# Turning four groups of tokens before the first attention step, gate scores from an exponential, and a bias addition tied to its step

## The chip, the core and the metric

The kernel runs on one core of one Trainium2 chip. The core has a matrix engine (TensorE, PE in the profile, with its weight loads as PEld), a vector engine (VectorE, DVE), an engine for activation functions (ScalarE, ACT), a general engine (GpSimd, POOL) and a queue engine that only issues transfers here (SyncE, SP). The metric is the device time of one execution in microseconds, as the median of three runs.

## The reference

The kernel computes one transformer block on a tensor of 4 x 1024 tokens with 256 channels, in float32. Attention and a mixture of experts both read the same normalised input, and both are added to it:

```python
xn = layernorm(x)
x = x + attention(xn) + experts(xn)

def attention(x):                     # 16 heads of 16 channels
    q, k, v = split(x @ W_qkv + b_qkv)
    q, k = rotary(q), rotary(k)
    a = softmax(q @ k.T / sqrt(16))
    return (a @ v) @ W_out + b_out

def experts(x):                       # 16 experts in 4 groups of 4
    scores = sigmoid(x @ w_gate.T)
    # a group's score is the sum of its two best scores; the best 2 groups stay,
    # and of their 8 experts the best 4 (w, idx)
    w = w / (sum(w) + 1e-6)
    routed = sum over the 4: w * (silu(x @ w1_e.T) * (x @ w3_e.T)) @ w2_e.T
    shared = (silu(x @ w1_s.T) * (x @ w3_s.T)) @ w2_s.T
    return routed + shared
```

## The kernel before

**Steps.** The 4096 tokens are 32 tiles of 128, and 8 groups of 4 tiles (`QT = 4`). Attention is the backbone: 256 steps (`STEPS`), 16 for each of 16 pairs of a batch entry and four heads. A step takes four score matmuls `ps` (L1289) through an exponential on ScalarE (`es`, L1298), makes four matmuls `pm` (L1247) whose row maxima (`mx`, L1255, a VectorE reduction) the next pair needs, and multiplies earlier exponentials into the values (`av`, L1314). Four matmuls come in the first half and four in the second; `between()` places all other work of the step, its *units*, in the middle. `max_off` (L1266 to L1275) merges two maxima, transposes them on TensorE (`pmt`) and subtracts them from the queries (`q2`). Until it has run, a pair's exponentials can't begin.

**Before step 0.** Groups 0 and 1 are normalised and transposed (`turn`, L467 to L492: four transposes per half group on TensorE into a PSUM bank `pt`, one copy on ScalarE), the first batch entry's queries, keys and values are made in eight tiles, and the first maxima are taken: `max_round(0, 0, s)` for eight `s`. The even ones run within the tile loop, the odd ones after it. Meanwhile ScalarE and VectorE collect statistics of groups 2 to 7, and POOL turns them into scale and offset (`rstd`, `off`). `scale(q)` (L456) is four ScalarE activations that normalise group `q` in place.

**Groups 2 to 7.** `Norm.moves(step)` runs at the head of a step: it scales group `step + 3`, stores the rows of group `step + 2` to DRAM (`xnd`) and, from group 4, the transposed group to `xnTd`. `Norm.pieces(step)` puts the turns of group `step + 2` among the units, and in steps 3 and 5 the gate's matmuls for groups 2 to 5 and 6 and 7 (`pg`, L502). Their logits come a step later (`plg`, L518). In steps 0 to 6 the own pair's remaining maxima are units too.

**Routing.** `route` is a generator. From step 9 (`ROUTE_FROM`) it is advanced three times in a step, twice while the experts are ranked, and each advance runs to the next `yield`. It begins with the sigmoid of all logits (L608, 128x512) and the best two of each group (`hi`, `lo`, L616 and L618). `rank` (L630 to L637) compares with VectorE (`ge`, two buffers) and adds and subtracts on POOL (`rk`, L635 and L636) for 15 distances.

**Shared experts.** `shared_block` makes units for 16 blocks of 256 tokens. `gate(1)` holds a POOL addition of the output bias to the block's input rows `xb` (L875), which `last` uses two units later (L905). The rows are loaded by SP well ahead (`early_x`).

**Who sets the order.** A planner orders each engine's instructions by simulated readiness, unless they are tied. `keep_in_program_order` ties one behind everything traced so far on its engine, and all TensorE work and all SP transfers of `k.sp` are tied in this way. `issue_after(ins)` queues behind `ins` on its engine. `paced` adds a true wait on `k.pace`, the latest reduction or exponential that a step's hooks have passed. PSUM has eight banks from one pool (`k.bank`), and SBUF buffers are reused by tag.

Of the kernel before, what the change touches and what calls it, by code (L numbers as in the profile page):

```python
# [10 lines left out]
AF = mybir.ActivationFunctionType  # L11
# [9 lines left out]
NT = B * TT  # L21
# [7 lines left out]
HALF = 512  # L29
QT = 4  # L30
# [22 lines left out]
def kernel(  # L53
# [23 lines left out]
    nc = tc.nc  # L77
# [6 lines left out]
    k = Kit(tc, banks)  # L84
# [35 lines left out]
    logits = rt_pool.tile([P, NT, E], F32, name="logits", tag="logits")  # L120

    ff = ctx.enter_context(tc.tile_pool(name="ff", bufs=2))
    norm = Norm(k, att, ff, keep, logits, power)
# [44 lines left out]
    with tc.issue_after(k.rotary):  # L168
        for power_of in powers:
            power_of()  # L170
    norm.scale(2)
    for qt in range(4):
        att.max_round(0, 0, 2 * qt + 1)
    att.max_off(0, 0, 0)

    def weights():
        nc.scalar.dma_start(out=k.w1s_sb, in_=w1s.rearrange("(c p) f -> p c f", p=P))
        nc.scalar.dma_start(out=k.w3s_sb, in_=w3s.rearrange("(c p) f -> p c f", p=P))
        nc.scalar.dma_start(out=k.w2s_sb, in_=w2s.rearrange("(c p) h -> p c h", p=P))
        k.sp(wout_sb, w_out.rearrange("(c p) f -> p c f", p=P))  # L180
# [115 lines left out]
class Kit:  # L296


    def __init__(self, tc, banks):
        self.tc, self.nc, self.banks = tc, tc.nc, banks  # L300
        self.last_sp = self.last_exp = None
        self.ranking = self.slots_known = False
        self.summed = self.shared_rows = 0
# [26 lines left out]
class Norm:  # L330
# [3 lines left out]
    def __init__(self, k, att, ff, keep, logits, power):  # L334
        self.k, self.nc, self.att, self.ff = k, k.nc, att, ff
        self.logits, self.power = logits, power
        self.gates = {3: (2, 3, 4, 5), 5: (6, 7)}
        self.less = keep.tile([P, NT], F32, name="less")
        self.sq = keep.tile([P, NT], F32, name="sq")
        self.x4, self.xnT, self.part, self.lg = {}, {}, {}, {}  # L340
        self.mv, self.rstd, self.off, self.scaled = {}, {}, {}, None
# [28 lines left out]
    def power_of(self, q):  # L370
        nc, ff, mv = self.nc, self.ff, self.mv[q]
        rstd = self.rstd[q] = ff.tile([P, QT], F32, name=f"rstd_{q}", tag="rstd", bufs=8)
        keep = self.k.tc.keep_in_program_order
        keep(nc.gpsimd.tensor_scalar_add(mv[:, :, 1], mv[:, :, 1], 1e-5))
        keep(nc.gpsimd.tensor_tensor(rstd, mv[:, :, 1], self.power, ALU.pow))
# [76 lines left out]
    def scale(self, q):  # L452
        nc = self.nc
        for i in range(QT):
            x = self.x4[q][:, i, :]
            scale = nc.scalar.activation(  # L456
                x, x, AF.Identity,
                bias=self.off[q][:, i : i + 1], scale=self.rstd[q][:, i : i + 1],
            )
            if q < 4:  # L460
                self.k.tc.keep_in_program_order(scale)

    def store(self, q):
# [3 lines left out]
    def turn(self, q, pair):  # L467

        nc, k = self.nc, self.k
        b, hf = divmod(q, 2)  # L470
        if hf == 0 and pair == 0 and b < 2:
            self.xnT[b] = k.xnTp.tile([P, NC_, T], F32, name=f"xnT_{b}", tag="xnT")
        if pair == 0:
            if b < 2:
                self.part[q] = self.xnT[b][:, :, hf * HALF : (hf + 1) * HALF]
            else:

                self.part[q] = self.att.one.tile(
                    [P, NC_, HALF], F32, name=f"xnTq_{q}", tag=("oc", "acc")[hf]
                )  # L480
        pt = k.bank([P, NC_, 2, P], f"pt_{q}_{pair}")
        for i in range(2):
            for c in range(NC_):
                k.pe(
                    nc.tensor.transpose(  # L485
                        pt[:, c, i, :], self.x4[q][:, 2 * pair + i, c * P : (c + 1) * P], k.ident
                    )
                )
        nc.scalar.copy(
            self.part[q][:, :, pair * 2 * P : (pair + 1) * 2 * P],  # L490
            pt.rearrange("p c i n -> p c (i n)"),
        )  # L492

    def gate(self, qs):

# [35 lines left out]
    def moves(self, step):  # L531

        k = self.k
        q = step + 3
        if q < NT // QT:
            with k.tc.issue_after(k.last_exp or k.pace):
                self.scale(q)
        if step + 2 < NT // QT:
            self.store(step + 2)
        if 4 <= step + 1 < NT // QT:  # L540
            b, hf = divmod(step + 1, 2)
            k.sp(k.xnTd[b][:, :, hf * HALF : (hf + 1) * HALF], self.part[step + 1])

    def pieces(self, step, own):
        out = []
        if step + 2 < NT // QT:
            out += [lambda: self.turn(step + 2, 0), lambda: self.turn(step + 2, 1)]
        if own:
            out.append(own.pop(0))
        if step in self.gates:  # L550
            out.append(lambda: self.gate(self.gates[step]))
        if step - 1 in self.gates:
            out.append(lambda: self.logits_of(self.gates[step - 1]))
        return out + own


def route(k, one, logits, tensor):
# [5 lines left out]
    nc = k.nc  # L563
# [7 lines left out]
    with k.tc.issue_after(k.rotary):  # L571
# [3 lines left out]
            out=before, in_=before, compare_op=ALU.is_gt, fill=0.0, base=0,  # L575
# [20 lines left out]
        out=same, in_=k.ident.rearrange("p (t e) -> p e t", e=E), axis=AX.X, op=ALU.add  # L596
# [6 lines left out]
        out=late, in_=late, compare_op=ALU.is_gt, fill=0.0, base=-E * shift,  # L603
# [1 line left out]
    )  # L605

    sc = tile_([P, NT, E], "sc")
    k.tc.keep_in_program_order(nc.scalar.activation(sc, logits, AF.Sigmoid))  # L608
    yield


# [104 lines left out]
    while not ahead:  # L716
# [23 lines left out]
        out=lower, in_=lower, compare_op=ALU.is_gt, fill=0.0, base=0,  # L740
# [53 lines left out]
class Beside:  # L794
# [52 lines left out]
    def shared_block(self, blk):  # L847


        k, nc = self.k, self.nc  # L850
        b, at = divmod(blk * SL, T)
        st = {"gu": []}

        def half(c, n):
            ph = k.bank([P, SL], f"ph_s{blk}_{c}_{n}")
            w = (k.w1s_sb, k.w3s_sb)[n]
            for i in range(NC_):
                k.pe(
                    nc.tensor.matmul(  # L859
                        ph, lhsT=w[:, i, c * P : (c + 1) * P],  # L860
                        rhs=self.xnT[b][:, i, at : at + SL],
                        start=(i == 0), stop=(i == NC_ - 1),
                    )
                )
            return ph

        def gate(c):
            def run():
                if c == 0:
                    self.early_x(blk)  # L870
                    if blk + 1 not in (SHARED_FIRST, NT // R):
                        self.early_x(blk + 1)
                    st["x"] = self.xb[blk]
                else:
                    nc.gpsimd.tensor_tensor(  # L875
                        st["x"], st["x"], k.bo_sb.unsqueeze(1).to_broadcast([P, R, C]), ALU.add
                    )
                if at == 0 and c == 0:
                    self.want(b)
                ph = half(c, 0)  # L880
                th = st["th"] = self.ff.tile([P, SL], F32, name=f"th_s{blk}_{c}", tag="th")
                nc.scalar.activation(th, ph, AF.Tanh, scale=0.5)
                nc.vector.scalar_tensor_tensor(th, th, 1.0, ph, ALU.add, ALU.mult)
            return run

        def up(c):
            def run():
                ph = half(c, 1)
                gu = self.ff.tile([P, SL], F32, name=f"gu_s{blk}_{c}", tag="gu", bufs=3)
                nc.vector.tensor_tensor(gu, st["th"], ph, ALU.mult)  # L890
                st["gu"].append(gu)
            return run

        def last(r):
            def run():
                po = k.bank([P, C], f"pso_{blk}_{r}")
                for c in range(FS // P):
                    k.pe(
                        nc.tensor.matmul(  # L899
                            po, lhsT=st["gu"][c][:, r * P : (r + 1) * P], rhs=k.w2s_sb[:, c, :],  # L900
                            start=(c == 0), stop=(c == FS // P - 1),
                        )
                    )
                x = st["x"][:, r, :]
                nc.vector.scalar_tensor_tensor(x, po, 0.5, x, ALU.mult, ALU.add)  # L905
                if r == R - 1:
                    self.later.append(store)
            return run

        def store():  # L910
            k.sp(k.rows(k.acc, blk * R, R), st["x"])
            k.shared_rows = (blk + 1) * R

        return [gate(0), up(0), gate(1), up(1)] + [last(r) for r in range(R)]
# [655 lines left out]
```

## Time and profile before

| | us |
|---|---|
| median of three runs | 1413.76 |
| lowest and highest run | 1411.64, 1413.96 |
| the profiled execution | 1414.77 |
| its span, first to last instruction | 1413.1 |

The profiled execution's span leaves out 1.7 us of its time that lie around the instructions. Rows of the timeline begin with the start and the duration in us, then the engine, the line in the kernel, the operation, what it writes and reads with shapes, and how many instructions were merged; in brackets stands how long the engine was idle before, and what released it. Rows of the windows table begin with the stretch of time. A kind like `qkT` is a buffer that several tensors share: groups 2 to 5 lie in buffers of the queries and keys that are needed only later. `granted clock` is the share of full speed that TensorE was allowed.

### The profile page before, as it was taken

The numbers are of one execution on the slowest core, as the hardware profiler recorded it, in microseconds if no ns is written. First come the engines' busy times: TensorE is split into PE (matmuls) and PEld (weight loads), VectorE is DVE, ScalarE is ACT, GpSimd is POOL, SyncE is SP. The second block draws the span as 40 slices with busy tenths as digits, with TensorE's granted clock in tenths as the row PEclk, the third lists the DMA queues.
The fourth block names the chain that finished last, engine by engine and source line by source line (L and its number), as shares of the span: only waits on it lengthen the run. The fifth ranks groups of instructions, "written<-read, shape, count | busy, mean of one in ns | idle before, by whom it ended". The sixth has DMA issues, their size and how long they took to land.

```text
span 1413.1 us, 25832 instructions
## 1 busy us (share of the span) xinstructions
PE 1389.0 (98%) x9446; PEld 653.6 (46%) x9446; DVE 931.0 (66%) x1734; ACT 783.6 (55%) x1586; POOL 424.7 (30%) x498
## 2 busy tenths in 40 slices
PE   7899999999999999999999999999999999999998
PEld 4443333343343335566566665665664333333333
DVE  6778758778777765444555555555447988998941
ACT  4564445565555555555555555555555555555575
POOL 5401603764444454220000000002225444444400
PEclk9899999999999999999999999999999999999999
DMA  5143743413332333547666666665432434433310
GB/s 187 45 150 134 283 165 104 142 68 105 120 120 104 99 135 95 172 153 230 210 203 201 202 202 213 197 200 174 150 120 75 125 107 128 127 108 105 109 38 31
DMA packets 136670, 199.10 MB, mean 141 GB/s; under 512 B 13920, under 2 KB 99040, under 8 KB 136288
## 3 DMA queue, kind: packets, MB, share of 16 engines
q1 hardware_dynamic: 103088, 137.78, 30.7%
q0 software_dynamic: 12288, 33.57, 7.7%
q10 hardware_dynamic: 21168, 26.10, 5.3%
q8 instruction: 75, 1.23, 0.4%
q14 instruction: 51, 0.42, 0.1%
HBM read 124.01 MB, written 79.69 MB: 144 GB/s over the span
## 4 chain that ended last, share of the span: by engine, by line
PE 97%; DVE 1%; DMA 1%; ACT 1%; issue 0%; POOL 0%; ACTq 0%; POOLq 0%; DVEq 0%
PE ps L1289 20%; PE pm L1247 20%; PE av L1314 18%; PE ph_r L827 9%; PE exy L994 5%; PE ph_s L859 5%; PE pqk L1161 4%; PE py L1383 2%; PE pso L899 2%; PE pv L1161 2%; PE ext L985 2%; PE ptr L1228 2%; PE pmt L1270 1%; PE po L1338 1%; DVE mx L1255 1%; PE pt L485 1%
## 5 line engine op out<-in xcount | busy, mean ns | idle before, releaser
L1298 ACT ACTIVATE es<-ps 128x512 f32<-128x512 f32 x1024 | 554.9, 596 | 460.3 <-PE ps L1289 238.4
L1255 DVE TENSOR_REDUCE mx<-pm 128x1 f32<-128x512 f32 x1024 | 661.3, 685 | 193.9 <-PE pm L1247 139.0
L1247 PE MATMUL pm<-kT,qT 32*128 32x512 f32 x1792 | 513.1, 646 | 1.4 <-ACT kT L1233 1.4
L1289 PE MATMUL ps<-q,kT 32*128 32x512 f32 x1792 | 509.3, 643 | 3.1 <-DVE mx L1255 2.2
L1314 PE MATMUL av<-es,vv 128*32 128x512 f32 (+1 forms) x2144 | 277.3, 588 | 0.0
L1289 PEld LDWEIGHTS ps<-q,kT 32*128 32x128 f32 x1792 | 142.5, 184 | 192.5 <-ACT es L1298 135.0
L1247 PEld LDWEIGHTS pm<-kT,qT 32*128 32x128 f32 x1792 | 147.5, 185 | 67.6 <-DVE mx L1255 30.0
L835 DVE SCALAR_TENSOR_TENSOR th_r<-th_r,ph_r 128x256 f32<-128x256 f32 x72 | 30.3, 421 | 199.6 <-ACT th_r L834 199.6
L950 POOL DMA_INDIRECT xs<-rows,slot_i x128 | 124.0, 969 | 114.7 <-DVE mx L1255 101.5
L1042 POOL DMA_INDIRECT yg<-ys,slot_i x128 | 121.5, 949 | 121.8 <-DVE mx L1255 115.8
L1192 POOL TENSOR_TENSOR rot<-qk,sin_sb 128x256 f32<-128x256 f32 x56 | 39.5, 728 | 348.4 <-DVE qk L1149 348.2
L827 PE MATMUL ph_r<-xT,w 128*128 128x128 f32 x1152 | 140.5, 275 | 0.5 <-ACT xT L988 0.5
L1314 PEld LDWEIGHTS av<-es,vv 128*32 128x32 f32 x2144 | 43.1, 108 | 199.9 <-issue 178.1
L827 PEld LDWEIGHTS ph_r<-xT,w 128*128 128x128 f32 x1152 | 134.4, 192 | 0.8 <-ACT xT L988 0.7
L994 PE MATMUL exy<-w,gu_r 128*128 128x256 f32 x288 | 76.6, 388 | 0.0
L834 ACT ACTIVATE th_r<-ph_r 128x256 f32<-128x256 f32 x72 | 27.7, 384 | 82.6 <-PE ph_r L827 82.6
L1289 PE MATMUL ps<-q,qkT 32*128 32x512 f32 x256 | 72.7, 640 | 0.0
L1247 PE MATMUL pm<-qkT,qkT 32*128 32x512 f32 x256 | 72.6, 640 | 0.0
L994 PEld LDWEIGHTS exy<-w,gu_r 128*128 128x128 f32 x288 | 50.6, 190 | 28.9 <-issue 21.7
L1059 DVE SCALAR_TENSOR_TENSOR sum<-yg,wk,sum 128x256 f32<-128x256 f32 x128 | 63.6, 496 | 0.4 <-DMA yg<-ys,slot_i 0.4
L1000 ACT ACTIVATE y<-exy 128x512 f32<-128x512 f32 x72 | 43.2, 600 | 35.0 <-PE exy L994 29.9
L875 POOL TENSOR_TENSOR xb<-xb,bo_sb 128x512 f32<-128x512 f32 x16 | 20.9, 1308 | 90.4 <-DMA xb<-in_x_dram 76.4
(178 smaller groups left out, 1210.3 us busy)
## 6 DMA issues: line engine op xcount, KB each, us to landing
w<-we SPq DMA_DIRECT2D x144, 384.0 KB, 3.8
xs<-zero ACTq DMA_DIRECT2D x8, 2304.0 KB, 7.9
xg<-xs SPq DMA_DIRECT2D x72, 256.0 KB, 4.8
ys<-y SPq DMA_DIRECT2D x72, 256.0 KB, 4.7
acc<-acc SPq DMA_DIRECT2D x14, 512.0 KB, 5.2
xb<-in_x_dram SPq DMA_DIRECT2D x16, 256.0 KB, 4.2
acc<-xb SPq DMA_DIRECT2D x16, 256.0 KB, 3.2
we<-in_w_dram ACTq DMA_DIRECT2D x4, 1024.0 KB, 7.3
```

Of the source, the lines that this page charges most:

```text
L827: nc.tensor.matmul(ph[:, n, at], lhsT=w[n][:, c, :], rhs=xT[:, c, at], start=(c == 0), stop=(c == NC_ - 1),)
L859: nc.tensor.matmul(ph, lhsT=w[:, i, c * P : (c + 1) * P], rhs=self.xnT[b][:, i, at : at + SL], start=(i == 0), stop=(i == NC_ - 1),)
L950: put = nc.gpsimd.indirect_dma_start(out=k.xs, out_offset=bass.IndirectOffsetOnAxis(ap=k.slot_i[:, t, kk : kk + 1], axis=0), in_=self.rows ...
L994: nc.tensor.matmul(py[:, r, :], lhsT=gus[i][:, r * P : (r + 1) * P], rhs=got[i][1][:, r, 2 * NC_ * F :], start=True, stop=True,)
L1042: get = nc.gpsimd.indirect_dma_start(out=self.yg[:, kk, :], out_offset=None, in_=k.ys, in_offset=bass.IndirectOffsetOnAxis(ap=k.slot_i[:, ...
L1059: nc.vector.scalar_tensor_tensor(sm[:, 0, :], yg[:, kk, :], k.wk[:, t, kk : kk + 1], sm[:, 0, :], ALU.mult, ALU.add)
L1161: nc.tensor.matmul(ps, lhsT=self.xnT[b][:, c, t * P : (t + 1) * P], rhs=self.wqkv_sb[:, c, at : at + w], start=(c == 0), stop=(c == NC_ - 1),)
L1247: nc.tensor.matmul(ps, lhsT=self.qT[b, g // 2][rows, g % 2, qt * P : (qt + 1) * P], rhs=self.kT[b, g // 2][rows, g % 2, hf * HALF : (hf + ...
L1255: k.pace = nc.vector.tensor_reduce(out=self.mx_of[b, g, qt // 4][hf][:, qt % 4, j, :], in_=ps, axis=AX.X, op=ALU.max,).ins
L1289: nc.tensor.matmul(ps, lhsT=self.kT[b, g // 2][rows, g % 2, kc * P : (kc + 1) * P], rhs=self.q2[b, g, qh][rows, :], start=True, stop=True,)
L1298: k.last_exp = nc.scalar.activation(e, ps, AF.Exp, scale=DH**-0.5).ins
L1314: nc.tensor.matmul(av[32 * j : 32 * j + 32, cols], lhsT=self.vv[b][:, kc, h * VS : h * VS + 32], rhs=es[j][:, cols], start=(kc == 0), stop ...
```

## The change

The turns of groups 2 to 5, with the scalings of groups 3 to 5, move before step 0, between and behind the odd rounds of the first maxima; their scalings and copies are tied into ScalarE's order. Groups 6 and 7 are scaled at steps 0 and 1 and turned in steps 2 and 3, the gate's matmuls move to steps 1 and 4, and the stores of transposed groups 4 to 7 to steps 0, 1, 3 and 4. The gate's scores are computed as 1 / (1 + exp(-logit)) by an exponential on ScalarE, an addition and a reciprocal on VectorE; four yields are added. The bias's addition waits for the step's pace instruction.

```diff
     norm.scale(2)
+    norm.scale(3)
+
     for qt in range(4):
         att.max_round(0, 0, 2 * qt + 1)
+        if qt == 1:
+            norm.turn(2, 0)
+            norm.scale(4)
+        if qt == 2:
+            norm.turn(2, 1)
+    for q in (3, 4):
+        for pair in range(2):
+            norm.turn(q, pair)
+    norm.scale(5)
     att.max_off(0, 0, 0)
+    for pair in range(2):
+        norm.turn(5, pair)
...
-        self.gates = {3: (2, 3, 4, 5), 5: (6, 7)}
+
+        self.turns, self.gates = {2: 6, 3: 7}, {1: (2, 3, 4, 5), 4: (6, 7)}
...
-            if q < 4:
+            if q < 6:
                 self.k.tc.keep_in_program_order(scale)
...
-        nc.scalar.copy(
+        copy = nc.scalar.copy(
             self.part[q][:, :, pair * 2 * P : (pair + 1) * 2 * P],
             pt.rearrange("p c i n -> p c (i n)"),
         )
+        if 2 <= q < 6:
+            k.tc.keep_in_program_order(copy)
...
-        q = step + 3
+        q = step + 6
         if q < NT // QT:
             with k.tc.issue_after(k.last_exp or k.pace):
                 self.scale(q)
         if step + 2 < NT // QT:
             self.store(step + 2)
-        if 4 <= step + 1 < NT // QT:
-            b, hf = divmod(step + 1, 2)
-            k.sp(k.xnTd[b][:, :, hf * HALF : (hf + 1) * HALF], self.part[step + 1])
+        q = step + 4 if step < 2 else self.turns.get(step - 1)
+        if q:
+            b, hf = divmod(q, 2)
+            k.sp(k.xnTd[b][:, :, hf * HALF : (hf + 1) * HALF], self.part[q])
...
-        if step + 2 < NT // QT:
-            out += [lambda: self.turn(step + 2, 0), lambda: self.turn(step + 2, 1)]
+        if step in self.turns:
+            out += [lambda i=i: self.turn(self.turns[step], i) for i in range(2)]
...
-    k.tc.keep_in_program_order(nc.scalar.activation(sc, logits, AF.Sigmoid))
+    k.tc.keep_in_program_order(nc.scalar.activation(sc, logits, AF.Exp, scale=-1.0))
+    yield
+    yield
+    yield
+    nc.vector.tensor_scalar_add(sc, sc, 1.0)
+    yield
+    nc.vector.reciprocal(sc, sc)
     yield
...
-                    nc.gpsimd.tensor_tensor(
+                    plus = nc.gpsimd.tensor_tensor(
                         st["x"], st["x"], k.bo_sb.unsqueeze(1).to_broadcast([P, R, C]), ALU.add
                     )
+                    k.paced(plus.ins)
```

## The prediction

> **What bounds the kernel now.** I read the page's busy shares first, then TensorE by stage (windows), then its waits, then the timelines around each bad stage.
>
> ```profile
> PE 1389.0 (98%) x9446; PEld 653.6 (46%) x9446; DVE 931.0 (66%) x1734; ACT 783.6 (55%) x1586; POOL 424.7 (30%) x498
> 46.00:61.00 15.00, 9.91 (x42) 4.44 (x40) 12.52 (x22) 6.18 (x17) 10.77 (x46) 0.76 0.28 88
> 120.00:142.00 22.00, 20.79 (x112) 6.98 (x105) 17.64 (x42) 12.42 (x21) 5.13 (x4) 0.84 0.58 214
> 168.00:182.00 14.00, 11.80 (x68) 3.74 (x68) 7.46 (x17) 4.84 (x9) 4.60 (x11) 0.88 0.61 221
> 182.00:300.00 118.00, 118.00 (x730) 45.91 (x734) 87.65 (x149) 63.81 (x131) 50.56 (x51) 1.00 0.41 135
> ```
>
> The columns are the window, its length, busy us of PE, PEld, DVE, ACT and POOL, then the granted clock. From 182 us on TensorE is busy at clock 1.00, and nothing edited there is on its path. The change can pay only in three stages: 46 to 112 us (first maxima and steps 0 to 6), 120 to 142 (gate scores, steps 9 to 12), 168 to 182 (step 19).
>
> ```profile
> 48.06 4.12 ACT L456 ACTIVATE qkT<-qkT,off,rstd 128x256 f32<-128x256 f32 x8
> 49.18 9.66 DVE L1255 TENSOR_REDUCE mx<-pm 128x1 f32<-128x512 f32 x16 [1.16 <-PE pm L1247]
> 59.12 1.12 PE L1270 MATMUL pmt<-ident,mx 128*128 128x128 f32 x4 [2.93 <-DVE mx L1266]
> 61.08 1.22 PE L1289 MATMUL ps<-q,kT 32*128 32x512 f32 x1 [0.85 <-DVE q L1275]
> 54.00:56.00 2.00, 2.00 (x5) 0.50 (x2) 2.00 (x5) 0.00 (x0) 1.75 (x6) 0.50 0.85 244
> 64.00:66.00 2.00, 2.00 (x10) 1.19 (x12) 0.52 (x1) 1.43 (x3) 0.00 (x0) 0.50 0.00 0
> ```
>
> In the first stage the sixteen reductions set the pace (9.66 us, 0.604 each), ScalarE is idle after 52.2, and the clock is halved from about 53.8 to 67.4.
>
> ```profile
> 121.47 1.28 ACT L608 ACT_TABLE_LOAD   x1
> 122.76 0.63 ACT L608 ACTIVATE sc<-logits 128x512 f32<-128x512 f32 x1
> 123.41 1.28 ACT L1298 ACT_TABLE_LOAD   x1
> 124.71 2.56 ACT L1298 ACTIVATE es<-ps 128x512 f32<-128x512 f32 x5
> 124.25 2.88 POOL L875 TENSOR_TENSOR xb<-xb,bo_sb 128x512 f32<-128x512 f32 x2
> 124.52 1.49 DVE L618 TENSOR_TENSOR lo<-sc 128x256 f32<-128x256 f32 x1
> 171.91 1.26 POOL L875 TENSOR_TENSOR xb<-xb,bo_sb 128x512 f32<-128x512 f32 x1 [5.37 <-DMA xb<-in_x_dram]
> 175.06 1.12 PE L1289 MATMUL ps<-q,kT 32*128 32x512 f32 x2 [2.20 <-DVE mx L1255]
> ```
>
> Two table loads surround the sigmoid, and five exponentials pile up behind them. Two early bias additions on POOL stretch `lo` (its twin `hi` took 0.42). At 166.5 POOL stands 5.4 us behind a bias addition whose rows have not landed, with the ranks of L635 queued behind it. VectorE then waits for a rank buffer, and TensorE for VectorE.
>
> **Part one, the turns.** Nothing disappears; work moves. One group costs four scalings (2.06 us on ACT, half of the row of eight), eight transposes (1.09 on TensorE when warm, 1.97 when cold) and two copies (1.07 on ACT). Groups 2 to 5 leave steps 0, 1, 2, 3, and groups 6 and 7 go from steps 4, 5 to 2, 3.
>
> New stretch before step 0, from 48.06: ACT scales groups 2 and 3 to 52.2 as now, copies (52.8), scales group 4 (its offset is ready at 52.6) to 54.9, makes five copies to about 58.3 and scales group 5 to 60.4. TensorE has all matmuls of the maxima out by about 55.5, since 8 PSUM banks hold at most 8 results and ACT frees the turns' banks. The reductions should therefore still end at 58.84. All turns but group 5's hide under them. Group 5's stand between the maxima's transposes and step 0, ending about 61.7: step 0 begins 0.6 late. Without that cover the four groups would cost 4 x 1.97 on TensorE and more on ACT.
>
> Steps 0 to 6 start now at 61.1, 68.1, 75.7, 82.1, 89.3, 97.3 and 104.1, and step 7 at 111.9 (first `ps` of each in the timeline): 50.8 us. I rebuild each from warm pieces: a half step 1.07, full `av` 1.06, own round of maxima 1.15 (VectorE: eight reductions, 4.83), gate 1.92, logits 0.66. Step 0 cold without its turn: 5.9; step 1 with the gate 6.4; step 2 with turn and logits 6.2; step 3 with turn 5.6; step 4 with gate 6.4; step 5 5.4; step 6, twelve reductions, 7.5. Sum 43.4, so 7.4 saved, less the 0.6: **6.8**. Only 4.4 of it is TensorE work; the rest is scalings that now stand between exponentials in steps 1 to 4. Lower end 3.0, if those stalls come back as VectorE backlog. Upper end 8.5.
>
> A rule bears against this. The Trainium skill, "TensorE: Matmul & The Clock Gate", part on PE-mode transpose, says that transposes do not count as PE activity for the clock. Row 54:56 agrees with the general idea (PE 2.00 of 2.00 busy, clock 0.50), but shows thin matmuls and not transposes. If transposes counted, step 0 could start warm and about 2 us more would come. I follow the rule and leave step 0 cold.
>
> DMAs: the stores of groups 4 and 5 to `xnTd` go out at steps 0 and 1, those of 6 and 7 at steps 3 and 4. SP takes them in order, and store(3) and `wout_sb` stand behind them, some 10 us before `fold` needs the latter: nothing. On POOL the powers stay in place.
>
> **Part two, the gate scores.** Two loads of 1.28 leave ACT: 2.6. "ScalarE: Activation LUTs", What ACT_TABLE_LOAD costs, puts a drain of 1.38 beside each load, which would make 5.3 for two switches. The trace has the next ACTIVATE 1.29 and 1.30 after each load, so I take 2.6. VectorE gains an addition (0.42, as the 128x512 TENSOR_SCALAR of L664) and a 128x512 reciprocal that no row shows. RECIPROCAL took 250 ns at 128x16 and 343 at 128x32: 5.8 ns per element, hence 343 + 480 x 5.8 = 3.1. Ends: 0.7 (an ordinary pass of that width) and 5.5 (16 times the row of 32); I take 3.1, the slope. It stands in step 10 between reductions, and the rest of routing slips four yields.
>
> Steps 9 to 12 take 22.4 now (119.7 to 142.1; steps 10 and 11 alone 13.7, mostly cold). After: step 9 4.3. Steps 10 and 11: VectorE has eight reductions 5.2, addition and reciprocal 3.5, nine small passes and `q` 3.6, 12.3 in all; TensorE runs ahead by the free banks, about 2 us: 10.3. Step 12 5.1. One cold window of 3.4 costs 1.2. Sum 20.9, gain 1.5; the long reciprocal would turn it into a loss of 1. I take **1.0**, range -3 to 4.
>
> **Part three, the bias's addition.** The added wait is on the step's pace instruction, a reduction or an exponential that has just been issued; behind it on POOL stand that step's ranks, later the row puts, which TensorE does not wait for. Block 2's addition leaves step 19: the stall of 2.2 goes, and the cold window after it (176.6 to 180.0, half speed: 1.7): **3.6**, leaving 0.3 to what is late next. Block 0's addition comes into step 14, where now three rank rounds fall together (7.6 us of POOL for the first three in the trace, plus 1.3). Ranks have two buffers, so VectorE waits near step 15, some 2.6 less the banks' slack: **loss 1.0**, range 0 to 3. The other additions run beside a VectorE that is 66% busy: nothing.
>
> **Sum.** 6.8 + 1.0 + 3.6 - 1.0 = 10.4. The profiled execution took 1414.8 (span 1413.1), 1.0 above the median of 1413.8: 1404.4 on its scale, **1403.4** on the median's.
>
> **Rivals.** (a) As above, 0.60: 1400 to 1407. (b) The moved work buys only its TensorE time and VectorE becomes the bound, 0.20: 4.4 - 0.6 from turns, -2 for the reciprocal with two cold windows, 3.6 - 1.0: 4.4, so 1409.4. For it: reductions already end the wait of `ps` and `pmt`. Against: VectorE is 66% busy, and ACT has 29.9 us of work in 61 to 112. (c) Slower, 0.12: POOL holds VectorE off at every tied addition. `lo` lost 1.07 beside one, and sixteen now sit within busy steps. All of it on TensorE's path would be 17.1, less 10.4: 1420.5. It cancels the gain from 0.65 each and shows as slower from 0.83. Against: from 182 us on, thirteen additions run today without a TensorE wait. (d) The planner had the order so already, or the added ties bring other waits as large as the ones removed, 0.08: 1413.
>
> About 0.2% (2.8 us) is what a measurement can tell from no change. Faster: all of (a), most of (b): 0.79. Same: the rest of (b), most of (d) and the mild end of (c): 0.11. Slower: 0.10. Leaving out the low end and (c) gives 1399.5 to 1412.
>
> **What would show it.** Right: step 7 starts near 105 on the old scale; four L456 groups before 61; no table load at the gate; one RECIPROCAL of about 3 us; L875 after its step's ranks and no 2.2 us wait at step 19. Wrong: reductions of the first stage with gaps, `ps` of step 0 later than 63, clock 0.5 over more than one window in steps 10 to 12, or POOL's L875 in front of a late reduction in many steps.

## The result and the profile after

| | before | after |
|---|---|---|
| median of the runs of this comparison, us | 1412.70 (4 runs) | 1420.87 (4 runs) |
| lowest and highest run, us | 1411.53, 1413.96 | 1420.32, 1421.18 |
| profiled execution, us | 1414.77 | 1420.75 |
| its span, us | 1413.1 | 1419.0 |

The ratio is 1.0054, with a 95% interval of 1.004 to 1.0067. The changed kernel is slower, by about 8 us; a gain of 10 was forecast.

The page's busy shares hardly move. The windows do (window, length, busy time of PE, PEld, DVE, ACT and POOL, granted clock, DMA share, GB/s):

```profile
PE 1384.9 (98%) x9454; PEld 651.4 (46%) x9454; DVE 933.3 (66%) x1736; ACT 781.8 (55%) x1584; POOL 425.6 (30%) x498
46.00:61.00 15.00, 1.14 (x9) 0.86 (x8) 2.52 (x5) 4.37 (x14) 10.93 (x45) 0.69 0.00 0
179.00:193.00 14.00, 14.00 (x92) 5.06 (x88) 10.47 (x23) 7.00 (x13) 4.05 (x11) 1.00 0.81 290
```

Between 46 and 61 us TensorE now works 1.14 us of 15, where it worked 9.91. The last row is the stage around step 19, which the changed kernel reaches 11 us later (180.9 for 169.8): TensorE is busy throughout, where it worked 11.80 us of 14. TensorE's waits name the cause of the first; the fields are the engine, what it waited to write, whom for, us in total, times and the longest. The first line is of before, the others are of after:

```profile
PE pm L1247 <- ACT kT L1233: 1.4, 1, 1.4
...
PE pm L1271 <- ACT kT L1257: 14.5, 1, 14.5
PE pmt L1294 <- DVE mx L1290: 1.4, 1, 1.4
PE po L1362 <- DVE q L1299: 1.1, 1, 1.1
PE ps L1313 <- DVE mx L1279: 0.9, 1, 0.9
```

The wait for ScalarE's copy `kT` has grown from 1.4 us to 14.5. The timeline of ScalarE, with one row of POOL ahead of it, says what the copy stood behind:

```profile
56.40 0.20 POOL L435 TENSOR_TENSOR off<-less,rstd 128x4 f32<-128x4 f32 x1
...
56.63 1.09 ACT L470 ACTIVATE x<-x,off,rstd 128x256 f32<-128x256 f32 x2 [11.06 <-POOL off L435]
57.63 0.62 ACT L1257 COPY qT<-ptr 128x256 f32<-128x256 f32 x2
58.15 0.65 ACT L1257 COPY kT<-ptr 128x256 f32<-128x256 f32 x2
...
59.67 1.09 ACT L470 ACTIVATE x<-x,off,rstd 128x256 f32<-128x256 f32 x2
60.65 0.64 ACT L1257 COPY qT<-ptr 128x256 f32<-128x256 f32 x2
61.17 0.67 ACT L1257 COPY kT<-ptr 128x256 f32<-128x256 f32 x2
```

L470 is `scale`, and its rows that write `x` and not `qkT` belong here to group 6. Two of its four activations stand ahead of one tile's query and key copies, two ahead of the next tile's. The first pair waits 11.06 us for group 6's offset, which POOL has only at 56.6. The queries and keys of the last two tiles stand behind it, and behind those the whole first stage. On TensorE:

```profile
61.62 3.79 PE L1271 MATMUL pm<-kT,qT 32*128 32x512 f32 x16 [14.48 <-ACT kT L1257]
...
73.66 0.66 PE L1294 MATMUL pmt<-ident,mx 128*128 128x128 f32 x4 [1.39 <-DVE mx L1290]
74.15 1.35 PE L499 MATMUL pt<-ident,qkT 128*128 128x128 f32 x8
75.42 0.69 PE L1313 MATMUL ps<-q,kT 32*128 32x512 f32 x1
```

Step 0 begins at 75.42, not 61.08: **14.3 us late**. That is more than the whole loss.

To follow the rest I use one mark every eight steps, the start of ScalarE's copy `oT`; the first falls in step 9. Relative to the first profile of before, after stands at +6.96 in step 9, +10.61 in step 17, +6.79 in step 25 and +5.98 at the last mark. So steps 0 to 8 won back 7.4 of the 14.3, steps 9 to 17 lost 3.7, steps 18 to 25 won 3.8, and 0.8 more came late. In the gate's stage the new rows on VectorE, TensorE and POOL are these:

```profile
133.59 3.34 DVE L631 RECIPROCAL sc<-sc 128x512 f32<-128x512 f32 x1
...
137.54 0.66 PE L1362 MATMUL po<-ident,oT 128*128 128x128 f32 x4 [1.15 <-DVE q L1299]
...
160.09 1.27 POOL L898 TENSOR_TENSOR xb<-xb,bo_sb 128x512 f32<-128x512 f32 x1
...
163.90 0.56 DVE L657 TENSOR_TENSOR ge_e<-msk 128x384 f32<-128x384 f32 x1 [0.90 <-POOL rk L659]
...
165.12 1.12 PE L1313 MATMUL ps<-q,kT 32*128 32x512 f32 x2 [0.94 <-DVE mx L1279]
```

While the reciprocal runs, `q` waits for VectorE, and TensorE waits for `q`. Later block 0's addition stands between the first two rank rounds, VectorE waits 0.90 for a rank buffer, and TensorE 0.94 for VectorE.

### The profile page after: what moved, and what is told of

Its sections match the earlier page's. It is cut to its first block, busy times and chain, and to the rows that moved or that the text cites. A ratio compares the mean times of both kernels' runs of the same rounds, so it can differ in the third digit from the quotient of the medians.

```text
span 1419.0 us, 25853 instructions
## 1 busy us (share of the span) xinstructions
PE 1384.9 (98%) x9454; PEld 651.4 (46%) x9454; DVE 933.3 (66%) x1736; ACT 781.8 (55%) x1584; POOL 425.6 (30%) x498
## 4 chain that ended last, share of the span: by engine, by line
PE 95%; DVE 2%; POOL 1%; ACT 1%; DMA 0%; issue 0%; ACTq 0%; DVEq 0%; POOLq 0%
PE pm L1271 20%; PE ps L1313 20%; PE av L1338 18%; PE ph_r L850 9%; PE exy L1018 5%; PE ph_s L882 4%; PE pqk L1185 4%; PE pso L923 2%; PE py L1407 2%; PE ext L1009 2%; PE pv L1185 2%; PE ptr L1252 2%; PE po L1362 1%; PE pmt L1294 1%; PE pf L1395 1%; PE pt L499 1%
## 5 line engine op out<-in xcount | busy, mean ns | idle before, releaser
L1271 PE MATMUL pm<-kT,qT 32*128 32x512 f32 x1792 | 510.7, 644 | 14.6 <-ACT kT L1257 14.5
L1083 DVE SCALAR_TENSOR_TENSOR sum<-yg,wk,sum 128x256 f32<-128x256 f32 x128 | 61.5, 480 | 0.0
```

The source lines that it names most:

```text
L1083: nc.vector.scalar_tensor_tensor(sm[:, 0, :], yg[:, kk, :], k.wk[:, t, kk : kk + 1], sm[:, 0, :], ALU.mult, ALU.add)
L1271: nc.tensor.matmul(ps, lhsT=self.qT[b, g // 2][rows, g % 2, qt * P : (qt + 1) * P], rhs=self.kT[b, g // 2][rows, g % 2, hf * HALF : (hf + ...
```

## The experiments

Three causes were on trial: the scaling of group 6 at step 0, the gate's exponential with its reciprocal, and the tied bias addition. Runs sent together share runs of before on one chip. Before's own median was 1419.3, 1415.1 and 1422.1 us in the three sets, so ratios hold within a set only. The changed kernel ran beside the 1412.7 of the first comparison alone, so its loss of 8 belongs to that comparison. Across sets I compare traces, with the first profile of before where no other is named.

**Group 6 tied.** The changed kernel, with group 6's scaling in ScalarE's order too.

```diff
-            if q < 6:
+            if q < 7:
                 self.k.tc.keep_in_program_order(scale)
```

> The changed kernel with one number different: the scalings of group 6, too, are tied into ScalarE's order (q < 7 for q < 6). Theory A: the planner put group 6's untied scaling in front of the last copies of keys and queries, where it waits for an offset from POOL; nothing else delays the first maxima. Then TensorE's wait of 14.5 us on L1257 goes, step 0 starts at 61.7 (75.4 in the changed kernel), and the time falls by 13.7 to about 1407, 6 below the kernel before. Rival B: the turns and copies put between the maxima hold TensorE and ScalarE up by their own work; then the first maxima still come late and the time stays near 1421.

Measured: 1406.51 us (1406.06 to 1406.67), ratio to before 0.9907 [0.9894, 0.9921]. TensorE's wait and ScalarE's rows at that place are:

```profile
PE pm L1271 <- ACT kT L1257: 1.4, 1, 1.4
...
48.26 4.14 ACT L470 ACTIVATE qkT<-qkT,off,rstd 128x256 f32<-128x256 f32 x8
...
61.66 2.07 ACT L470 ACTIVATE x<-x,off,rstd 128x256 f32<-128x256 f32 x4
63.63 1.06 ACT L1322 ACTIVATE es<-ps 128x512 f32<-128x512 f32 x2
```

Group 6's activations now stand in one piece at 61.66, just ahead of step 0's exponentials. Step 0 starts at 61.06 and step 7 at 104.50. One number in the code is worth 14.6 us of span (1419.0 to 1404.4), and turns the loss into a gain: 0.9% by the medians of this set, 0.6% by the traces (1404.4 for 1413.1). Theory A's time of about 1407 was met.

**Group 6 untied in the kernel before.** Before, with only this added: group 6 is scaled at step 0 beside group 3, and later groups as before.

```diff
-        q = step + 3
-        if q < NT // QT:
+        for q in {0: (3, 6), 1: (4,), 2: (5,), 4: (7,)}.get(step, ()):
```

> The kernel before, with group 6 scaled untied at step 0 instead of at step 3, and no turn moved. Theory A: the same four activations land before the last copies, the first maxima come 13 to 14 us late, 1426 to 1427. Rival B (the moved turns do it): no turn is moved, so the time stays at 1413, or falls a little because step 3 loses four activations.

Measured: 1435.40 us (1429.94 to 1437.45), ratio 1.0101 [1.0078, 1.0124].

```profile
PE pm L1246 <- ACT kT L1232: 14.5, 1, 14.5
...
56.30 1.09 ACT L456 ACTIVATE x<-x,off,rstd 128x256 f32<-128x256 f32 x2 [11.04 <-POOL off L421]
```

The same 14.5 and the same 11 us appear in a kernel in which no turn has moved. At the step 9 mark it stands 13.9 behind before, as theory A had it. The time is 16 above before's in this set, for the 13 to 14 expected, and the last mark is 21.5 behind; the further 7.6 grow over many steps and are not located.

**Turns alone.** Part one, with group 6 tied; the sigmoid and the untied addition are kept. Shown against the changed kernel.

```diff
-            if q < 6:
+            if q < 7:
...
-    k.tc.keep_in_program_order(nc.scalar.activation(sc, logits, AF.Exp, scale=-1.0))
...
-    nc.vector.tensor_scalar_add(sc, sc, 1.0)
...
-    nc.vector.reciprocal(sc, sc)
+    k.tc.keep_in_program_order(nc.scalar.activation(sc, logits, AF.Sigmoid))
...
-                    k.paced(plus.ins)
```

> Part one alone on the kernel before, with group 6 tied: turns and scalings moved, sigmoid and bias addition as before. Theory A with the sum of the prediction: steps 0 to 6 take 43.4 for 50.8, start 0.6 later, so 1413 - 6.8 = 1406, and the stages from step 9 on are as before. Rival B: slower than before by up to 14.

Measured: 1411.31 us (1406.77 to 1412.80), ratio 0.9933 [0.9916, 0.995]. At step 9 it is 7.6 ahead, and at the last mark 3.2: the turns' gain is there, and some of it is lost again in steps where the bias is not tied. The time is 8 below before's in this set, for the 7 expected.

**Gate scores alone.** Part two in the kernel before.

```diff
-    k.tc.keep_in_program_order(nc.scalar.activation(sc, logits, AF.Sigmoid))
+    k.tc.keep_in_program_order(nc.scalar.activation(sc, logits, AF.Exp, scale=-1.0))
     yield
+    yield
+    yield
+    nc.vector.tensor_scalar_add(sc, sc, 1.0)
+    yield
+    nc.vector.reciprocal(sc, sc)
+    yield
```

> Part two alone on the kernel before: exponential, addition and reciprocal for the sigmoid, four more yields; turns and bias addition as before. The changed kernel loses 3.65 us between steps 9 and 17. Theory C: the long reciprocal and the three rank rounds that now fall together in step 14 do that; then this kernel is 2 to 4 slower than before, 1415 to 1417, with a new wait in steps 15 to 16. Rival D: the bias addition of block 0 among the ranks does it; then this kernel is the same or up to 1.5 faster (two table loads of 1.28 less), 1411.5 to 1413.

Measured: 1424.39 us (1423.44 to 1427.63), ratio 1.004 [1.0025, 1.0055]. It stands at 0.00 at the step 9 mark, +3.5 in step 17 and +8.7 at the last mark, a larger loss than the 2 to 4 of theory C. A wait of its TensorE that before does not have:

```profile
PE po L1344 <- DVE q L1281: 2.1, 1, 2.1
```

What part two costs beside a tied bias does not follow from this run and the turns'; later runs show it.

**A second profile of before**, unchanged, to see how far two executions differ by themselves.

> The kernel before once more, unchanged, for a profile on the same chip as the experiments: there it took 1414.8 to 1421.7 in eleven runs, against 1411.5 to 1414.0 in the first four. Theory E: POOL's untied bias additions stand in front of ranks and row puts while their rows are still on the way, so the time hangs on when transfers land; then the second profile shows stalls behind L875 at other places or of other lengths than the first. Rival: the spread comes from the clock windows alone; then the stages from 200 us on last as long as in the first profile.

Measured: 1412.27 us, span 1410.6; it ran on the chip of the second set, not of the first. By step 17 it is 2.7 ahead of the first profile of before, of which 2.2 came in steps 9 to 17; from there on it keeps 2.5. From 200 us on it lasts as long as the first profile, which is the rival's sign. The 2.2 lie where the clock differs (the first profile, then the second):

```profile
124.00:136.00 12.00, 10.79 (x47) 3.82 (x48) 9.57 (x26) 5.53 (x10) 3.14 (x3) 0.72 0.71 265
124.00:136.00 12.00, 10.79 (x64) 3.72 (x60) 10.88 (x29) 6.28 (x12) 2.69 (x2) 1.00 0.74 276
```

TensorE is idle for the same 1.21 us in both. In the first profile a share of 0.72 makes 6.7 us at half clock, and in the second there is none. So a difference of 2 us in those steps, between one trace of before and another kernel's, proves nothing alone.

**Bias addition alone.** Part three in the kernel before.

```diff
-                    nc.gpsimd.tensor_tensor(
+                    plus = nc.gpsimd.tensor_tensor(
...
+                    k.paced(plus.ins)
```

> Part three alone on the kernel before: the bias addition waits for its step's pace. By the prediction's step: 3.6 us saved at step 19 and up to 1.0 lost near step 15; and `lo` beside no addition, so steps 9 to 12 get 1 to 2 shorter. Theory E adds that the run-to-run spread falls below 1 us. So 3 to 6 faster than before. Rival D (an addition among the ranks costs more than it saves): 0 to 2 faster, with a VectorE wait for POOL at steps 14 to 16.

Measured: 1407.76 us (1407.65 to 1407.90), ratio 0.995 [0.9937, 0.9964]: 7 faster, and with a spread of 0.25 us over five runs, where before's nine runs in this set spread over 5.4. That is 1 more than theory E's range. The trace ends 7.0 ahead of the first profile of before and 4.5 ahead of the second. POOL's waits for the rows are gone. Of before:

```profile
POOL xb L875 <- DMA xb<-in_x_dram: 76.4, 9, 42.9
```

No such line is among the waits of the kernel with the tied addition.

**Turns and bias, with the sigmoid.** The changed kernel with group 6 tied and part two undone.

```diff
-            if q < 6:
+            if q < 7:
...
-    k.tc.keep_in_program_order(nc.scalar.activation(sc, logits, AF.Exp, scale=-1.0))
+    k.tc.keep_in_program_order(nc.scalar.activation(sc, logits, AF.Sigmoid))
...
-    nc.vector.tensor_scalar_add(sc, sc, 1.0)
...
-    nc.vector.reciprocal(sc, sc)
```

> The tied kernel of e1 with the sigmoid back in: parts one and three without part two. Theory C (the long reciprocal and three rank rounds in one step cost the 3.6 us between steps 9 and 17): 3 to 5 faster than e1, 1401.5 to 1403.5. Rival F (the two table loads of 1.28 cost as much as the reciprocal): within 1 of e1, 1405.5 to 1407.5.

Measured: **1400.54 us** (1400.20 to 1403.66), ratio 0.9906 [0.989, 0.9921]: the shortest time of all, 1 below theory C's range. Its stage from 124 to 130 us against that of the kernel with all three parts and group 6 tied (first row: with the sigmoid; second: with the exponential):

```profile
124.00:130.00 6.00, 5.99 (x34) 2.04 (x30) 5.07 (x14) 2.66 (x5) 0.00 (x0) 1.00 0.65 241
```

```profile
124.00:130.00 6.00, 6.00 (x16) 1.35 (x15) 5.00 (x14) 1.20 (x2) 0.00 (x0) 0.66 0.52 192
130.00:136.00 6.00, 6.00 (x36) 2.31 (x36) 3.53 (x12) 2.56 (x5) 0.00 (x0) 0.77 0.05 17
```

With the sigmoid 34 matmuls end in that window, with the exponential 16, at a clock of 0.66. That share makes 4.1 us at half clock, and the 0.77 of the next row 2.8. The traces part there: equal at step 9 (0.05 us), 6.8 apart in step 17, 5.7 at the end. Part two costs about 6 us. This rests on the traces: the ratios of the two kernels, each to before in its own set, are alike (0.9906 and 0.9907).

**Reciprocal in quarters, routing a step earlier.** All three parts, group 6 tied. The second change keeps the steps that are open to the shared experts where they were, and there are two yields more in all.

```diff
-ROUTE_FROM = 9
+ROUTE_FROM = 8
...
-        room = not now or att.light(step) and ROUTE_FROM + 10 < step < TILES_FROM
+        room = not now or att.light(step) and ROUTE_FROM + 11 < step < TILES_FROM
...
     yield
     yield
-    yield
     nc.vector.tensor_scalar_add(sc, sc, 1.0)
     yield
-    nc.vector.reciprocal(sc, sc)
-    yield
+    for i in range(4):
+        part_of = sc[:, i * NT // 4 : (i + 1) * NT // 4, :]
+        nc.vector.reciprocal(part_of, part_of)
+        yield
```

> The tied kernel of e1 with the reciprocal cut into four of 128 columns, each behind its own yield, and routing begun one step earlier (step 8 for 9), so that no step holds three rank rounds. Theory C, reciprocal part: a quarter takes 0.9 us and fits between two reductions, so TensorE's wait of 1.1 behind `q` and the cold windows of steps 10 to 12 go, some 2 to 3 us; the rank part: a further 1 to 2 at steps 14 to 16. 1401.5 to 1403.5. Rival F: the same VectorE work in pieces costs the same, 1406 to 1407.

Measured: 1403.86 us (1403.64 to 1403.91), ratio 0.9922 [0.9909, 0.9936]. Each quarter takes 0.94 us. By the last mark it wins back 2.2 of the 5.7, and its time is just above theory C's range. So the length of one instruction is not all of the cost, or the early start costs something itself. Four runs bear on that.

**No reciprocal.** All three parts with group 6 tied, and in the place of the reciprocal a second addition; the scores are then exp(logit) + 1 + 1, so this kernel leaves the sigmoid out.

```diff
-    k.tc.keep_in_program_order(nc.scalar.activation(sc, logits, AF.Exp, scale=-1.0))
+    k.tc.keep_in_program_order(nc.scalar.activation(sc, logits, AF.Exp, scale=1.0))
...
-    nc.vector.reciprocal(sc, sc)
+    nc.vector.tensor_scalar_add(sc, sc, 1.0)
```

> All three parts with group 6's scaling in order, but the scores are exp(logit) plus two additions: the reciprocal (3.3 us on VectorE) becomes a second 128x512 addition (0.42 us), and the exponential takes plus instead of minus its input. Yields are those of the full change, so routing starts its comparisons four yields late. This leaves the sigmoid's form out of the computation; the order of the scores is kept. Theory R (the reciprocal's length costs: TensorE idle 1.2 us and then halved for about 3 us): no clock below 0.9 in the steps 9 to 12, time 1402 to 1403.5 where the full change with that order took 1406.5. Theory S (the slip of routing past block 0's bias addition costs): 1405.5 to 1407.

**Slip alone.** Turns and bias with the sigmoid, and four empty yields behind it.

```diff
     k.tc.keep_in_program_order(nc.scalar.activation(sc, logits, AF.Sigmoid))
     yield
+    yield
+    yield
+    yield
+    yield
```

> Turns in order and the tied bias with the sigmoid kept (1400.5 before), and four empty yields behind the sigmoid, so that routing slips as it does with the exponential, and nothing else changes. Theory R: 1400.5 to 1402, with the ranks' wait of step 15 as the only new one. Theory S: 1404 to 1406.5, and a TensorE wait near step 15 of 0.9 us with VectorE behind POOL's rk.

Measured: 1402.80 us (1402.24 to 1403.29; ratio 0.9863 [0.9842, 0.9884]) without the reciprocal, inside theory R's range, and 1403.69 (1402.70 to 1404.83; 0.9872 [0.985, 0.9893]) with the slip alone, between the two ranges. By their marks against the sigmoid kernel (turns and bias):

| us behind the sigmoid kernel | step 9 | step 17 | last mark |
|---|---|---|---|
| slip alone | 0.50 | 3.84 | 2.31 |
| exponential, no reciprocal | 0.83 | 3.76 | 2.22 |
| exponential and reciprocal | 0.05 | 6.82 | 5.67 |

Both theories hold, each for a part. At the end the slip of four yields costs 2.3, of which 0.5 stood there at step 9 already, and the reciprocal another 3.4 (5.67 less 2.22). The switch of the activation table is not seen as a gain: the kernel without the reciprocal has two additions of 0.42 us on VectorE where the kernel with the slip has two table loads, and they stand within 0.1 us of each other at the end. With the slip alone, the wait near step 15 is the one of the changed kernel, and here the clock falls behind it:

```profile
141.58 1.26 POOL L896 TENSOR_TENSOR xb<-xb,bo_sb 128x512 f32<-128x512 f32 x1
...
145.38 0.56 DVE L655 TENSOR_TENSOR ge_e<-msk 128x384 f32<-128x384 f32 x1 [0.90 <-POOL rk L657]
...
146.60 1.32 PE L1311 MATMUL ps<-q,kT 32*128 32x512 f32 x2 [0.94 <-DVE mx L1277]
...
146.00:148.00 2.00, 1.40 (x6) 0.44 (x10) 1.54 (x4) 0.00 (x0) 1.84 (x3) 0.85 0.94 343
148.00:150.00 2.00, 2.00 (x12) 0.34 (x12) 1.31 (x3) 0.60 (x1) 1.92 (x2) 0.50 0.00 0
150.00:152.00 2.00, 2.00 (x11) 0.88 (x11) 0.56 (x1) 0.60 (x2) 1.84 (x3) 0.80 0.00 0
```

The three shares make 3.4 us at half clock. In the kernel with all three parts and group 6 tied the same wait of 0.94 ends at 150.71, and the clock stays up:

```profile
148.00:154.00 6.00, 5.01 (x24) 1.64 (x24) 4.12 (x10) 1.28 (x3) 5.61 (x6) 1.00 0.67 245
```

So the 2.3 and the 3.4 do not add up from the same stretches: one kernel lost clock behind the reciprocal, the other behind the ranks.

**The early start, twice.** All three parts with group 6 tied and the reciprocal whole; and turns and bias with the sigmoid. Both start routing in step 8.

```diff
-ROUTE_FROM = 9
+ROUTE_FROM = 8
...
-        room = not now or att.light(step) and ROUTE_FROM + 10 < step < TILES_FROM
+        room = not now or att.light(step) and ROUTE_FROM + 11 < step < TILES_FROM
```

> All three parts with group 6's scaling in order, reciprocal whole, routing from step 8 and not 9: three of the four slipped yields are given back. Theory R: the idle TensorE and the halved clock stay and move one step ahead, 1405 to 1406.5. Theory S: most of the loss is back, 1401 to 1403. The kernel with the reciprocal in quarters and the same start took 1403.9: equal to it means that quartering did nothing.

> Turns in order and the tied bias with the sigmoid kept, routing from step 8. Theory R: nothing to give back, 1399.5 to 1401.5. Theory S: an earlier start moves the ranks further ahead of block 0's addition, 1398 to 1400.

Measured: 1409.20 us (1404.48 to 1411.57), ratio 0.9906 [0.9885, 0.9927], and 1402.68 (1401.57 to 1404.40), ratio 0.9863 [0.9841, 0.9885]. Both are slower than either theory allowed, and the first's runs spread over 7 us. At step 9 the two stand 2.4 and 3.4 behind the sigmoid kernel, but 2.4 and 1.1 of that are there when step 0 begins (63.42 and 62.09 for 61.02), before any routing. What the early start itself costs shows in steps 9 to 12 with the sigmoid: 21.0 us for 18.9. In the first, TensorE's longest wait in these steps stands behind the reciprocal, now a step earlier, as theory R had it; the addition `bo_sb` follows it on VectorE:

```profile
117.40 3.34 DVE L631 RECIPROCAL sc<-sc 128x512 f32<-128x512 f32 x1
...
121.08 0.69 PE L1313 MATMUL ps<-q,kT 32*128 32x512 f32 x1 [2.15 <-DVE bo_sb L1240]
```

**Lengths by stage.** A step begins with its first `ps`, which is every eighth `ps` of the trace. Steps 7 and 8 take 7.79 us in every trace named here, so the lengths can be compared across sets. The forecast's row follows from the terms of its sum.

| us | step 0 begins | steps 0-6 | 9-12 | 13-16 | 19-20 |
|---|---|---|---|---|---|
| before | 61.1 | 50.8 | 22.4 | 19.1 | 13.1 |
| before, second profile | 61.6 | 49.8 | 20.2 | 19.1 | 13.3 |
| forecast | 61.7 | 43.4 | 21.4 | 20.1 | 9.5 |
| after | 75.4 | 43.4 | 23.4 | 21.8 | 9.0 |
| after, group 6 tied | 61.1 | 43.4 | 23.2 | 21.9 | 9.0 |
| bias alone | 61.5 | 49.8 | 18.9 | 20.1 | 8.9 |
| turns and bias, sigmoid | 61.0 | 43.4 | 18.9 | 19.5 | 8.9 |
| the same with the slip | 61.5 | 43.4 | 18.8 | 22.9 | 9.0 |
| no reciprocal | 61.8 | 43.4 | 18.3 | 23.0 | 9.0 |
| reciprocal in quarters, from step 8 | 61.6 | 43.4 | 22.2 | 20.6 | 9.0 |
| reciprocal whole, from step 8 | 63.4 | 43.4 | 22.4 | 22.9 | 8.9 |
| sigmoid, from step 8 | 62.1 | 43.4 | 21.0 | 19.4 | 8.8 |

The quarters shorten steps 9 to 12 hardly at all against the whole reciprocal with the same start (22.2 for 22.4). They gain in steps 13 to 16, where two more yields also move the ranks; what does it there is not separated.

## Why the prediction was wrong

**The step that failed: "step 0 begins 0.6 late".** It began 14.3 late. The change scales group 6 at step 0, and the prediction's list of ScalarE's work before step 0 does not have it: scalings of the later groups are costed only as work "between exponentials". The tie covers `q < 6`. Group 6's only other hold is `issue_after(k.last_exp or k.pace)`, which queues behind an instruction on that instruction's own engine. At step 0 no exponential exists and the pace instruction is a VectorE reduction, so nothing held the activations on ScalarE. The planner set them ahead of `qT` and `kT`, where they wait for POOL. With the tie the delay is gone, and without it the kernel before gets it too: the cause is shown. How the planner came to that place is only argued. The prediction's own sign, "`ps` of step 0 later than 63", came true at 75.42. The trace of after ends 6.0 behind before for a forecast of 10.4 ahead; 13.7 of these 16.4 are this step.

**Turns, 6.8 after the 0.6.** Steps 0 to 6 were summed to 43.4 us, and every trace with the turns moved has 43.4. The sum was right, in part by luck, since its pieces erred both ways: with group 6 tied step 0 took 4.2 us where 5.9 was put, and steps 1, 3 and 5 took 6.9, 6.5 and 5.7 where 6.4, 5.6 and 5.4 were put. The first goes with the clock. I weighed the Trainium skill's rule that transposes do not count for the clock ("TensorE: Matmul & The Clock Gate", PE-mode transpose) and left step 0 cold. With the turns between the maxima the clock was 1.00 there:

```profile
54.00:56.00 2.00, 2.00 (x11) 0.81 (x9) 2.00 (x5) 1.40 (x3) 1.83 (x5) 1.00 0.03 8
64.00:66.00 2.00, 1.87 (x12) 1.14 (x12) 2.00 (x5) 1.27 (x4) 0.00 (x0) 1.00 1.01 291
```

These rows are of the kernel with group 6 tied; before had 0.50 in both. The measurement decides against the cold step 0. That transposes alone would hold the clock is not shown, as matmuls of the maxima run among them.

**Gate scores, gain 1.0.** In the prediction's own terms steps 9 to 12 took 23.4 for 22.4, a loss of 1.0 and inside its range. But with the bias tied and the sigmoid kept they take 18.9, so part two costs 4.4 there, and with the slip about 6 by its end. The reciprocal was sized well (3.1, measured 3.34), the table loads did leave, and TensorE stood for 1.15 us, near what 3.34 less a run-ahead of 2 leaves. The term that was mis-sized is the clock: I had allowed "one cold window of 3.4", costing 1.2, and the rows from 124 to 136 of the kernel with group 6 tied add up to 6.8 us at half clock. The 2.6 us on ScalarE bought nothing that these runs show.

**Rank rounds and block 0's addition, loss 1.0.** The mechanism was right, with the place and the wait named. Steps 13 to 16 took 21.8 for 19.1: 2.7, near the upper end of the range. The wait is 0.94 of it; the rest is not placed. The clock stayed at 1.00 behind it.

**Step 19, 3.6.** Steps 19 and 20 took 9.0 for 13.1: 4.1. This term was right. Wrong is what stands beside it, that the other additions are worth nothing. With the bias alone tied, steps 9 to 12 take 18.9 for 22.4: `lo` takes 0.42 where it took 1.49, and the clock never falls.

```profile
123.92 0.42 DVE L618 TENSOR_TENSOR lo<-sc 128x256 f32<-128x256 f32 x1
...
120.00:142.00 22.00, 21.61 (x128) 8.13 (x124) 20.12 (x49) 13.96 (x23) 5.44 (x5) 1.00 0.76 281
```

Of these 3.5 us, 2.2 are missing from the second profile of before as well, so whether the tie brings them is open. The prediction had read `lo` beside POOL and did not carry it into this sum.

**The rivals.** The slower one stood at 1420.5, and the result is 1420.87, but its mechanism, POOL holding VectorE off at each tied addition until the whole kernel is slower, is refuted: the ties alone make the kernel faster. A number that fits does not confirm its story. With group 6 tied, the trace ends 8.7 ahead of before, for the 10.4 forecast.

## What to carry to other kernels

When a step is moved to an earlier place, look at what holds it there, for each instance: a tie that names its range, and a hold on "the latest of X" that is empty before X has begun. A stall of TensorE costs its own length and, at times, a stretch at half clock behind it. A wait of 1.15 us was followed by 6.8 us of it and a wait of 0.94 by none in one kernel and 3.4 in another, so put a range on it, and not one value. Before adding a long instruction to the engine that makes a step's inputs, compare its length with the time by which the consumer can run ahead, and not with the engine's share of busy time.

## What the runs showed of the hardware

A 128x512 RECIPROCAL on VectorE takes 3.34 us and a 128x128 one 0.94, where an addition of 128x512 takes 0.42. The granted clock stayed at 1.00 through the turns, where before fell to 0.50 in the same stage. Idle time of 1.21 us between 124 and 136 us was followed by half clock in one profile of before and not in the other. A 128x416 comparison on VectorE took 1.64 us while POOL ran block 0's addition and a rank round (first row, after), and 0.98 beside POOL's rank round (second row, before):

```profile
160.17 1.64 DVE L657 TENSOR_TENSOR ge_e<-msk 128x416 f32<-128x416 f32 x1
...
146.12 0.98 DVE L634 TENSOR_TENSOR ge_e<-msk 128x416 f32<-128x416 f32 x1
```

The bias addition tied alone repeats far more closely (0.25 us over five runs) than before (5.4 over nine), but kernels that add the turns to it spread over 3.5 and 7.1 us (the sigmoid kernel, and the whole reciprocal from step 8). That landing times of the rows make before's spread is not shown. In the second set it goes with the clock: before's runs with a mean granted clock of 0.994 or 0.995 took 1412.1 to 1413.4 us, and those with 0.990 or 0.991 took 1414.6 to 1417.5.
